# Four graph attention layers on one core: order and shape of the first loads and of the zero rows

## The chip, the core and the metric

The kernel runs on one core of one Trainium2 chip. The core has a matrix engine (TensorE, PE in the profile, with its weight loads as PEld), a vector engine (VectorE, DVE), an activation engine (ScalarE, ACT), GpSimd (POOL) and a queue engine that mostly issues transfers (SyncE, SP). ACT and POOL issue transfers too. Transfers of all three run on the core's 16 DMA engines. The metric is the device time of one execution in microseconds (us), the median of several runs; lower is better.

## The reference, cut to what matters

There are 4096 nodes with 256 features and one adjacency matrix for all four layers. Each layer normalises the nodes, applies ReLU, projects them, and replaces each node by a softmax-weighted sum over its neighbours, which is added to the node. Layer 0 has biases, layer 1 an ELU, layer 2 four heads, layer 3 a positive and a negative attention.

```python
h = jnp.maximum(_layernorm(x, axis=-1), 0.0)
x = x + _L0_gnn_ref(h, adj, L0_gnn_W, ...)   # layer 0; layers 1, 2, 3 in the same form
# inside a layer
h = node_features @ W.T + b_W
e = (h @ a1)[:, None] + (h @ a2)[None, :] + b_a[0]
e = jnp.where(e > 0, e, 0.2 * e)
attention = jax.nn.softmax(jnp.where(adjacency_matrix > 0, e, NEG_INF), axis=1)
h_prime = attention @ h
```

`adj` is int32, 4096 x 4096 (64 MB), and most of it is zero: the edge probability falls with the node's number, so that later nodes have few neighbours.

## The kernel before, in words

**Two paths.** `list_layers` (L468) does the work. A flag at its end says whether the lists that it built were long enough; if not, `dense_layers` would run. With these inputs the flag is zero, and only `list_layers` counts.

**Layer 0 is dense.** The targets are cut into NIB = 8 blocks of 512, the sources into NT = 32 tiles of 128. `block(ib)` (L1185) makes one `Unit` per block, with 32 steps, one for each source tile `jt`. Four source tiles are a chunk (CH = 4). At a chunk's first step `get` (L1189) issues the loads of the *next* chunk's adjacency (`load`, L1170: two transfers `s_raw` of 512 KB in the order of the SP queue, four buffers), turns this chunk's integers into bytes on DVE (L1201, `s_m`, or `mpre` for chunk 0), and, after chunk 0, writes them to DRAM as `mask_t` (L1203). Each step then needs the node tile's projected row `g[:, jt, :]`, so it forces the node work forward until `L0.ready[jt]` holds.

**A step's pipeline.** `run` (L1111) walks the plan with LEAD = (0, 2, 3, 6): a step is fetched at position p, weighed on DVE three positions later (L952, `s_p` = max of the two branches times the mask), and multiplied on PE six positions later (L988, `s_acc`). After each step it lets the queue `posts` move on by two parts and `lists_q` by one or two.

**Node work.** `node_rows` (L647) treats two tiles: statistics on DVE (L657, L658), 1/sqrt on ACT (L661, L662) and DVE (L673 to L675), the centred and clipped rows `s_z` (L666), the addition of the layer's bias to `x` on POOL (L670), two transposes per tile on PE (L680), and `project` (L693), which multiplies by the layer's weights `L.w` on PE (L702, `s_pj`) and scales the result on ACT (L713 to L737). It is a generator; a `yield` hands control back, and a number after it asks for that delay in the planner's own clock. `target_rows` (L873) makes `s_grow` for a block out of the scores of its four tiles.

**Weights.** `weights(l, pool, prep)` (L521) issues a layer's loads on the ACT queue (`s_w` L566, `s_wt` L574, `s_av` L576), and then at once the small products `s_wa` on PE (L580) and their copies into `L.w` on DVE (L592); for layer 0 also the bias row (L596 to L616). The tile `s_wt` has one buffer, so layer 1's waits for layer 0's to be used.

**The start of phase 0** (L1127 to L1230) is the part that the change touches. In order: all eight loads of `x` (512 KB each, 1 KB a row) on the ACT queue, with layer 0's weights after the first of them; layer 1's weights with their products; the constants of the list builder on POOL; then the zero rows. The zero rows are one extra row, number HALF = 2048, in each of the eight `mask_t` and in the three `table`s of layers 1 to 3, which the lists' empty places point at. They are written from POOL with 128 partitions of 4 bytes for each `mask_t` (L1145), and with 43 or 44 partitions of 24 or 48 bytes for each `table` (L1150). After that the first adjacency chunk is loaded, all 16 pairs of node tiles are put into `posts`, and `run` begins.

**After phase 0** the lists of neighbours are built between the blocks (`list_sources`, L773, with gathers of mask columns on POOL), and layers 1 to 3 take the first 512 targets densely and the others by their lists (L1243 on). These parts are not touched, save that `weights` has another signature.

The program's order gives the priority, and the compiler may put a ready instruction of an engine ahead of one that waits. Once placed, the instructions of one engine, and the transfers issued from one queue, start in their order.

Of the kernel before, what the change touches and what calls it, by code (L numbers as in the profile page):

```python
# [17 lines left out]
P = 128  # L18
# [449 lines left out]
def list_layers(ctx: ExitStack, tc: tile.TileContext, a: dict, out: bass.AP, flag):  # L468
# [49 lines left out]

    layers = {}

    def weights(l, pool, prep):  # L521

        L = layers[l] = Layer()
        L.l = l
        L.H, L.part = LH[l], PART[l]

        ncols = D + 3 * L.H + (D if l == 3 else 0)
        L.w = pool.tile([P, 2, ncols], F32, name=f"s_w{l}", tag=f"s_w{l}")
        L.s = small.tile([P, NT, L.H], F32, name=f"s_s{l}", tag=f"s_s{l % 2}", bufs=1)
        L.ready = [False] * NT  # L530
        L.bias = None
        L.table = table[l]
        q = nc.scalar
        if l == 2:
            for h in range(HEADS):
                q.dma_start(
                    L.w[:, :, h * DH : (h + 1) * DH],
                    a["L2_gnn_W"][h].rearrange("(c p) o -> p c o", p=P),
                )
            wt = prep.tile([DH, HEADS, D], F32, name="s_wt2", tag="wt")  # L540
            q.dma_start(wt, a["L2_WT"].rearrange("h o i -> o h i"))
            av = prep.tile([DH, HEADS, 2], F32, name="s_av2", tag="av")
            q.dma_start(av, a["L2_av"])
            ps = ps_mm.tile([P, 2, 2 * HEADS], F32, name="s_wa2", tag="mm")
            for c in range(2):
                for h in range(HEADS):
                    nc.tensor.matmul(
                        ps[:, c, 2 * h : 2 * h + 2],
                        lhsT=wt[:, h, c * P : (c + 1) * P],
                        rhs=av[:, h, :],  # L550
                        start=True,
                        stop=True,
                    )
            nc.vector.tensor_copy(L.w[:, :, D : D + HEADS], ps[:, :, 0 : 2 * HEADS : 2])
            nc.vector.tensor_copy(L.w[:, :, D + HEADS : D + 3 * HEADS : 2], ps[:, :, 1 : 2 * HEADS : 2])
            nc.vector.tensor_scalar(
                L.w[:, :, D + HEADS + 1 : D + 3 * HEADS : 2],
                ps[:, :, 1 : 2 * HEADS : 2],
                SLOPE - 1.0,
                None,  # L560
                op0=ALU.mult,
            )
            return L
        src, srcT = (("L0_WT", "L0_gnn_W"), ("L1_gnn_W", "L1_WT"), None, ("L3_gnn_W", "L3_WT"))[l]
        if l < 3:
            q.dma_start(L.w[:, :, 0:D], a[src].rearrange("(c p) o -> p c o", p=P))  # L566
        else:
            for k in range(2):
                q.dma_start(
                    L.w[:, :, k * (D + 6) : k * (D + 6) + D],  # L570
                    a["L3_gnn_wtrans"][k * D : (k + 1) * D, :].rearrange("(c p) o -> p c o", p=P),
                )
        wt = prep.tile([P, 2, D], F32, name=f"s_wt{l}", tag="wt")
        q.dma_start(wt, a[srcT].rearrange("(c p) i -> p c i", p=P))  # L574
        av = prep.tile([P, 2, 2], F32, name=f"s_av{l}", tag="av")
        q.dma_start(av, a[f"L{l}_av"])  # L576
        ps = ps_mm.tile([P, 2, 2], F32, name=f"s_wa{l}", tag="mm")
        for c in range(2):
            for k in range(2):
                nc.tensor.matmul(  # L580
                    ps[:, c, :],
                    lhsT=wt[:, k, c * P : (c + 1) * P],
                    rhs=av[:, k, :],
                    start=(k == 0),
                    stop=(k == 1),
                )
        for h in range(L.H):

            sign = (1.0, -1.0)[h]
            t = D + L.H + 2 * h  # L590
            for col, k, by in ((D + h, 0, sign), (t, 1, sign), (t + 1, 1, sign * (SLOPE - 1.0))):
                nc.vector.tensor_scalar(  # L592
                    L.w[:, :, col : col + 1], ps[:, :, k : k + 1], by, None, op0=ALU.mult
                )
        if l == 0:
            L.bias = prep.tile([1, D + 2], F32, name="s_bias0", tag="s_bias")  # L596
            q.dma_start(L.bias[:, 0:D], a["L0_bW_row"])
            ba = prep.tile([1, 1], F32, name="s_ba0", tag="ba")
            q.dma_start(ba, a["L0_ba"])
            bc = prep.tile([P, 2], F32, name="s_bc0", tag="bc")  # L600
            q.dma_start(bc, a["L0_bW_col"])
            pb = ps_mm.tile([1, 2], F32, name="s_pb0", tag="mm")
            for k in range(2):
                nc.tensor.matmul(
                    pb, lhsT=bc[:, k : k + 1], rhs=av[:, k, :], start=(k == 0), stop=(k == 1)
                )
            nc.vector.tensor_add(L.bias[:, D : D + 1], pb[:, 0:1], ba)
            nc.vector.tensor_copy(L.bias[:, D + 1 : D + 2], pb[:, 1:2])

            pb = ps_mm.tile([P, D + 2], F32, name="s_pbb", tag="mm")  # L610
            nc.tensor.matmul(pb, lhsT=ones[0:1, :], rhs=L.bias, start=True, stop=True)
            L.bias = const.tile([P, D + 3], F32, name="s_bias_all")
            nc.scalar.copy(L.bias[:, 0 : D + 2], pb)
# [3 lines left out]
        return L  # L617

# [28 lines left out]
    def node_rows(L, T0):  # L647
# [1 line left out]

        u = f"{L.l}_{T0}"  # L650
        tiles = (T0, T0 + 1)
        while any(stored[T] < L.l - 1 for T in tiles):
            yield
        mv = small.tile([P, 2, 2], F32, name=f"s_mv_{u}", tag="mv")
        for k, T in enumerate(tiles):
# [471 lines left out]
    with ExitStack() as phase:  # L1127
# [2 lines left out]
        stage = phase.enter_context(tc.tile_pool(name="s_stage", bufs=4))  # L1130
        mpool = phase.enter_context(tc.tile_pool(name="s_mask", bufs=5))
        gpool = phase.enter_context(tc.tile_pool(name="s_g0", bufs=1))
        for b in range(NIB):
            nc.scalar.dma_start(
                x[:, b * IT : (b + 1) * IT, :],
                a["x"][b * IB : (b + 1) * IB, :].rearrange("(c p) d -> p c d", p=P),
            )
            if b == 0:
                L0 = weights(0, prep, prep)
        L1 = weights(1, const, prep)  # L1140
        consts = list_constants(lists_p)
        zero_m = const.tile([P, 4], U8, name="zero_m")
        nc.gpsimd.memset(zero_m, 0.0)
        for b in range(NIB):
            nc.gpsimd.dma_start(mask_t[b][HALF : HALF + 1, :].rearrange("o (p k) -> (o p) k", k=4), zero_m)  # L1145
        zero = const.tile([P, 12], F32, name="zero")
        nc.gpsimd.memset(zero, 0.0)
        for l in (1, 2, 3):
            k = 12 if l == 3 else 6
            nc.gpsimd.dma_start(  # L1150
                table[l][HALF : HALF + 1, :].rearrange("o (p k) -> (o p) k", k=k), zero[0 : GW[l] // k, 0:k]
            )
        g0 = gpool.tile([P, NT, GW[0]], F32, name="g0")
# [10 lines left out]
        L1.pre = keep.tile([P, DP, GW[1]], F32, name="pre1")  # L1164
        L1.rows = rows_of(L1)
        half = CH // 2

        loaded = {}
# [1 line left out]
        def load(n):  # L1170

            ib, c = divmod(n, NCH)
            loaded[n] = []
            for h in range(2):
                raw = stage.tile([P, half, IB], I32, name=f"s_raw_{ib}_{c}_{h}", tag="raw")
                r0 = (c * CH + h * half) * P
                nc.sync.dma_start(
                    raw,
                    a["adjT"][r0 : r0 + half * P, ib * IB : (ib + 1) * IB].rearrange(
                        "(c p) i -> p c i", p=P  # L1180
                    ),
                )
                loaded[n].append(raw)

        def block(ib):  # L1185
            masks = {}
            seen = lists_p.tile([P, JT, IT], F32, name=f"seen_{ib}", tag="seen", bufs=2)

            def get(jt):  # L1189
                if jt % CH == 0:  # L1190
                    c = jt // CH
                    n = ib * NCH + c
                    if n + 1 < NIB * NCH:
                        load(n + 1)
                    m = (
                        mpre[:, :, ib * IB : (ib + 1) * IB]
                        if c == 0
# [21 lines left out]
                u.on_end = lambda: push(lists_q, list_sources(ib, seen, lists_p, consts))  # L1219
            return u  # L1220

        load(0)
        for T in range(0, NT, 2):
            push(posts, node_rows(L0, T))
        run([s for ib in range(NIB) for s in block(ib).plan()])
        push(lists_q, find_flag())
        while lists_q:
# [6 lines left out]
    gat = ctx.enter_context(tc.tile_pool(name="s_gather", bufs=9))  # L1234
    stream = ctx.enter_context(tc.tile_pool(name="s_stream", bufs=3))
    for l in (2, 3):
        L = weights(l, late, prep)
        L.pre = late.tile([P, DP, GW[l]], F32, name=f"pre{l}")
        L.rows = rows_of(L)
    for l in (1, 2, 3):  # L1240
        layers[l].big = late
    plan = []
# [147 lines left out]
```

## Time and profile before

| | |
|---|---|
| time | 1915.78 us (median of 3; 1912.8 to 1916.86) |
| span of the profiled execution | 1907.4 us |
| PE busy | 1753.6 us, 92% |
| PEld busy | 1481.6 us, 78% |
| DVE busy | 1361.7 us, 71% |
| POOL busy | 984.0 us, 52% |
| ACT busy | 606.4 us, 32% |
| moved by DMA | 253.30 MB, mean 133 GB/s |

The busy shares are means over the whole span. The profile also cuts the span into 40 equal slices (47.7 us each) and gives each engine's busy share in tenths, follows the chain of work that ended last, lists each line's instructions with what they waited for, and gives the bytes that the DMA engines moved in any stretch. A PE record's length includes its overlap with its neighbours, so a stretch's PE time is best read from how many matmuls start in it.

### The profile page before, as it was taken

How to read it: one execution, taken by the hardware profiler on the slowest of the kernel's cores; microseconds unless marked ns; L12 is line 12 of the kernel's file. 1: busy time of each engine (PE TensorE's matmuls, PEld its weight loads, DVE VectorE, ACT ScalarE, POOL GpSimd, SP SyncE). 2: the span in 40 equal slices, each digit the busy share in tenths (PEclk: the TensorE clock that was granted, in tenths of full speed). 3: DMA queues.
4: the chain of work that ended last, by engine and by line, in shares of the span. 5: the costliest groups of instructions: out<-in, count | busy, mean ns of one | idle time of the engine just before them, and what ended most of it. 6: DMA issues, size and time to landing. Idle time of an engine off the chain costs nothing.

```text
span 1907.4 us, 29989 instructions
## 1 busy us (share of the span) xinstructions
PE 1753.6 (92%) x9818; PEld 1481.6 (78%) x9818; DVE 1361.7 (71%) x3899; ACT 606.4 (32%) x1793; POOL 984.0 (52%) x962
## 2 busy tenths in 40 slices
PE   0299999999999888888889999999999999999997
PEld 0188888888888776667665778788999888888886
DVE  2286687787788434567668989989888466777775
ACT  0264111011011001123234776768999101111111
POOL 3120047754563376777764645444555177655542
PEclk9999999999999979999899999999999999999999
DMA  9832634753662233455432333333333366666653
GB/s 179 135 128 93 227 119 129 232 151 124 202 196 66 61 86 109 133 152 137 123 109 68 104 89 90 90 99 84 105 95 86 122 204 197 194 182 175 190 155 93
DMA packets 128760, 253.30 MB, mean 133 GB/s; under 512 B 22195, under 2 KB 51284, under 8 KB 128596
## 3 DMA queue, kind: packets, MB, share of 16 engines
q0 software_dynamic: 45696, 119.49, 23.6%
q1 hardware_dynamic: 74752, 125.23, 20.6%
q10 hardware_dynamic: 8148, 6.57, 2.3%
q8 instruction: 81, 1.33, 0.3%
q14 instruction: 83, 0.68, 0.1%
HBM read 215.32 MB, written 35.89 MB: 132 GB/s over the span
## 4 chain that ended last, share of the span: by engine, by line
PE 81%; DMA 8%; DVE 7%; issue 2%; ACT 1%; another core or an unknown queue 1%; POOL 1%; ACTq 0%; DVEq 0%; POOLq 0%
PE s_acc L988 50%; PE s_accm L1013 18%; PE s_pj L702 7%; DMA s_gg<-table,idx 4%; DVE s_p L952 3%; PE idx_ps L834 3%; DMA mask_t<-s_m 2%; PE s_sT L886 1%; PE s_tp L680 1%; DMA s_av<-in_L_av 1%; POOL s_gg L1289 1%; DVE first L828 1%; DVE s_st L657 0%; DVE s_p L961 0%
## 5 line engine op out<-in xcount | busy, mean ns | idle before, releaser
L1289 POOL DMA_INDIRECT s_gg<-table,idx x654 | 679.6, 1039 | 499.8 <-PE s_acc L988 191.5
L952 DVE SCALAR_TENSOR_TENSOR s_p<-s_grow,s_gg,mlist 128x128 f32<-128x128 f32 x1090 | 345.2, 346 | 187.1 <-DMA s_gg<-table,idx 128.2
L988 PE MATMUL s_acc<-g,s_p 128*128 128x257 f32 x2048 | 463.4, 382 | 0.0
L988 PEld LDWEIGHTS s_acc<-g,s_p 128*128 128x128 f32 x2048 | 384.9, 191 | 50.6
L847 POOL DMA_INDIRECT mlist<-mask_t,idx x218 | 265.5, 1218 | 277.5 <-DVE idx L844 214.4
L988 PE MATMUL s_acc<-s_gg,s_p 128*128 128x257 f32 x1308 | 310.0, 386 | 14.6 <-DVE s_p L952 14.2
L988 PEld LDWEIGHTS s_acc<-s_gg,s_p 128*128 128x128 f32 x1308 | 245.6, 192 | 60.3 <-DVE s_p L952 26.8
L952 DVE SCALAR_TENSOR_TENSOR s_p<-s_grow,g,s_m 128x512 f32<-128x512 f32 x224 | 166.4, 748 | 83.5 <-PE s_acc L988 64.1
L952 DVE SCALAR_TENSOR_TENSOR s_p<-s_grow,pre,mpre 128x128 f32<-128x128 f32 (+1 forms) x588 | 190.8, 364 | 43.0 <-PE s_acc L988 28.6
L1013 PE MATMUL s_accm<-s_p,s_gg 128*65 128x128 f32 x1744 | 202.5, 273 | 0.0
L938 ACT ACTIVATE s_p<-s_grow,s_minus,s_gg 128x128 f32<-128x128 f32 x436 | 187.1, 486 | 22.3 <-PE s_accm L1013 11.6
L1013 PEld LDWEIGHTS s_accm<-s_p,s_gg 128*65 128x65 f32 x1744 | 192.6, 138 | 1.9
L988 PE MATMUL s_acc<-pre,s_p 128*128 128x257 f32 x768 | 186.3, 387 | 0.6 <-DVE s_p L952 0.4
L892 ACT ACTIVATE s_grow<-s_sT 128x256 f32<-128x256 f32 (+2 forms) x127 | 45.1, 381 | 411.2 <-PE s_sT L886 361.6
L702 PE MATMUL s_pj<-s_w,s_hT 128*128 128x259 f32 (+3 forms) x640 | 168.8, 407 | 3.1 <-ACT s_g L737 2.6
L952 DVE SCALAR_TENSOR_TENSOR s_p<-s_grow,s_gs,s_ms 128x512 f32<-128x512 f32 x196 | 142.5, 747 | 38.5 <-PE s_accm L1013 18.0
L988 PEld LDWEIGHTS s_acc<-pre,s_p 128*128 128x128 f32 x768 | 145.3, 194 | 22.6 <-DVE s_p L952 0.9
L988 PE MATMUL s_acc<-s_gs,s_p 128*128 128x257 f32 x672 | 155.8, 385 | 0.2 <-DVE s_p L952 0.2
L702 PEld LDWEIGHTS s_pj<-s_w,s_hT 128*128 128x128 f32 x640 | 124.5, 202 | 27.3 <-ACT s_g L737 3.7
L988 PEld LDWEIGHTS s_acc<-s_gs,s_p 128*128 128x128 f32 x672 | 128.0, 192 | 21.4 <-DVE s_p L952 3.7
L1013 PE MATMUL s_accm<-s_p,pre 128*65 128x128 f32 (+1 forms) x928 | 120.6, 284 | 0.0
L1201 DVE TENSOR_SCALAR s_m<-s_raw 128x1024 uint8<-128x1024 int32 x112 | 78.0, 712 | 58.1 <-DMA s_raw<-in_adjT 57.4
(125 smaller groups left out, 1648.1 us busy)
## 6 DMA issues: line engine op xcount, KB each, us to landing
s_raw<-in_adjT SPq DMA_DIRECT2D x128, 512.0 KB, 5.6
mask_t<-s_m SPq DMA_DIRECT2D x56, 256.0 KB, 4.1
s_gs<-table SPq DMA_DIRECT2D x21, 516.0 KB, 5.7
s_gg<-table,idx POOLq DMA_INDIRECT x654, 3.4
table<-s_g SPq DMA_DIRECT2D x28, 258.0 KB, 2.3
s_ms<-mask_t SPq DMA_DIRECT2D x28, 256.0 KB, 3.6
x<-in_x ACTq DMA_DIRECT2D x8, 512.0 KB, 4.1
out<-s_out SPq DMA_DIRECT2D x32, 128.0 KB, 3.4
```

The lines of the kernel that those rows point to most:

```text
L680: nc.tensor.transpose(tp[:, c, :], zs[k][:, c * P : (c + 1) * P], ident)
L702: nc.tensor.matmul(ps, lhsT=hT[:, c, :], rhs=L.w[:, c, k * (D + 6) : k * (D + 6) + cols], start=(c == 0), stop=(c == 1),)
L828: nc.vector.tensor_tensor(first, place, lof[:, t, :].unsqueeze(1).to_broadcast([P, P, JT]), op=ALU.is_equal)
L834: nc.tensor.matmul(ps[:, 0:cap], lhsT=first[:, :, j], rhs=val[:, 0:cap, j * IT + t], start=(j == 0), stop=(j == JT - 1),)
L847: nc.gpsimd.indirect_dma_start(out=mlist[:, OFFS[T] + k, :], out_offset=None, in_=mask_t[ib], in_offset=bass.IndirectOffsetOnAxis(ap=idx[: ...
L892: nc.scalar.activation(grow[:, h1:h2, :], ps[:, h1 - h0 : h2 - h0].rearrange("p h a b -> p h (a b)"), AF.Exp, scale=scale,)
L938: nc.scalar.activation(w[:, h, :], u.grow[:, h, :], AF.Relu, scale=g[h][:, n - 1 : n], bias=minus)
L952: nc.vector.scalar_tensor_tensor(p[:, k, :], u.grow[:, h, :], g[k][:, n - 1 : n], m, op0=ALU.min if L.l == 3 and h == 1 else ALU.max, op1= ...
L988: nc.tensor.matmul(u.accs[it][h], lhsT=p[:, k, it * P : (it + 1) * P], rhs=g[k][:, 0:n], start=first, stop=last,)
L1013: nc.tensor.matmul(u.regions[h], lhsT=g[k][:, 0 : DH + 1], rhs=p[:, k, :],  start=first and (u.nt > 1 or h == 0), stop=last, skip_group_ch ...
L1201: nc.vector.tensor_scalar(m[:, h * half : (h + 1) * half, :], raw, 0.0, None, op0=ALU.is_gt)
L1289: nc.gpsimd.indirect_dma_start(out=g, out_offset=None, in_=L.table, in_offset=bass.IndirectOffsetOnAxis(ap=index[T][:, k : k + 1], axis=0),)
```

## The change

The change reorders and reshapes the start of phase 0.

- `weights` is split: it makes the tiles, and a generator `make_weights` first issues the loads on a queue `q` that the caller names, and after a `yield` does the products. A flag `L.made` says that the products are issued; `node_rows` of a layer waits for it.
- `x` is loaded block by block on the SP queue (`load_x`), and each block's two pairs of node tiles are put into `posts` with it. The order on SP is: x block 0, adjacency chunk 0, x blocks 1 to 3; x blocks 4 to 7 follow behind chunks 0 to 3 of the first block of targets.
- The zero rows are written at chunk 4 (`zero_rows`), on SP, from one partition: 512 bytes in one piece for each `mask_t`, and pieces of at most 258 floats (1032 bytes) for the tables: one, two (the second 24 bytes) and two.
- Layer 1's weights are loaded at chunk 5 on SP, and their products come into `posts` behind the node pairs.
- Layers 2 and 3 run their generators to the end where they did before.

It is meant to let the first matmuls start when their own inputs have come, without the transfers that are needed later.

```diff
-    def weights(l, pool, prep):
+    def weights(l, pool, prep, q):
...
-        q = nc.scalar
+        L.made = False
+        L.making = make_weights(L, pool, prep, q)
+        next(L.making)
+        return L
+
+    def make_weights(L, pool, prep, q):
+        l = L.l
...
         av = prep.tile([P, 2, 2], F32, name=f"s_av{l}", tag="av")
         q.dma_start(av, a[f"L{l}_av"])
+        if l == 0:
+            L.bias = prep.tile([1, D + 2], F32, name="s_bias0", tag="s_bias")
+            q.dma_start(L.bias[:, 0:D], a["L0_bW_row"])
...
+        yield 15.0
         ps = ps_mm.tile([P, 2, 2], F32, name=f"s_wa{l}", tag="mm")
...
-        return L
+        L.made = True
...
-        while any(stored[T] < L.l - 1 for T in tiles):
+        while any(stored[T] < L.l - 1 for T in tiles) or not L.made:
             yield
...
-        for b in range(NIB):
-            nc.scalar.dma_start(
+
+        def load_x(b):
+
+            nc.sync.dma_start(
                 x[:, b * IT : (b + 1) * IT, :],
                 a["x"][b * IB : (b + 1) * IB, :].rearrange("(c p) d -> p c d", p=P),
             )
-            if b == 0:
-                L0 = weights(0, prep, prep)
-        L1 = weights(1, const, prep)
-        consts = list_constants(lists_p)
-        zero_m = const.tile([P, 4], U8, name="zero_m")
-        nc.gpsimd.memset(zero_m, 0.0)
-        for b in range(NIB):
-            nc.gpsimd.dma_start(mask_t[b][HALF : HALF + 1, :].rearrange("o (p k) -> (o p) k", k=4), zero_m)
-        zero = const.tile([P, 12], F32, name="zero")
-        nc.gpsimd.memset(zero, 0.0)
-        for l in (1, 2, 3):
-            k = 12 if l == 3 else 6
-            nc.gpsimd.dma_start(
-                table[l][HALF : HALF + 1, :].rearrange("o (p k) -> (o p) k", k=k), zero[0 : GW[l] // k, 0:k]
-            )
+            for T in (b * IT, b * IT + 2):
+                push(posts, node_rows(L0, T))
+
+        def zero_rows():
+
+            zero = prep.tile([1, 2 * D], F32, name="zero", tag="wt")
+            nc.gpsimd.memset(zero, 0.0)
+            for b in range(NIB):
+                nc.sync.dma_start(mask_t[b][HALF : HALF + 1, :], zero[:, 0 : IB // 4].bitcast(U8))
+            for l in (1, 2, 3):
+                for k in range(0, GW[l], D + 2):
+                    n = min(D + 2, GW[l] - k)
+                    nc.sync.dma_start(table[l][HALF : HALF + 1, k : k + n], zero[:, 0:n])
+
+        L0 = weights(0, prep, prep, nc.scalar)
...
+        def behind(c):
+
+            if c + 4 < NIB:
+                load_x(c + 4)
+            if c == 4:
+                zero_rows()
+            if c == 5:
+                L1 = weights(1, const, prep, nc.sync)
+                L1.pre = keep.tile([P, DP, GW[1]], F32, name="pre1")
+                L1.rows = rows_of(L1)
+                push(posts, L1.making)
...
                     if n + 1 < NIB * NCH:
                         load(n + 1)
+                    if ib == 0:
+                        behind(c)
...
+        load_x(0)
         load(0)
-        for T in range(0, NT, 2):
-            push(posts, node_rows(L0, T))
+        for b in range(1, 4):
+            load_x(b)
+        consts = list_constants(lists_p)
+        for _ in L0.making:
+            pass
         run([s for ib in range(NIB) for s in block(ib).plan()])
```

More of the change, by code (lines that the diff above doesn't have):

```diff
@@ L562, in weights @@
             )
-            return L
+            L.made = True
+            return
         src, srcT = (("L0_WT", "L0_gnn_W"), ("L1_gnn_W", "L1_WT"), None, ("L3_gnn_W", "L3_WT"))[l]
@@ L576, in weights @@
         q.dma_start(av, a[f"L{l}_av"])
+        if l == 0:
+            L.bias = prep.tile([1, D + 2], F32, name="s_bias0", tag="s_bias")
+            q.dma_start(L.bias[:, 0:D], a["L0_bW_row"])
+            ba = prep.tile([1, 1], F32, name="s_ba0", tag="ba")
+            q.dma_start(ba, a["L0_ba"])
+            bc = prep.tile([P, 2], F32, name="s_bc0", tag="bc")
+            q.dma_start(bc, a["L0_bW_col"])
+        yield 15.0
         ps = ps_mm.tile([P, 2, 2], F32, name=f"s_wa{l}", tag="mm")
@@ L595, in weights @@
         if l == 0:
[L596 to L601, printed above, removed]
             pb = ps_mm.tile([1, 2], F32, name="s_pb0", tag="mm")
@@ L616, in weights @@
             )
-        return L
+        L.made = True
     posts, lists_q = [], []
@@ L1162, in rows_of @@
             return f
-        L1.pre = keep.tile([P, DP, GW[1]], F32, name="pre1")
-        L1.rows = rows_of(L1)
         half = CH // 2
@@ L1236, in list_layers @@
     for l in (2, 3):
-        L = weights(l, late, prep)
+        L = weights(l, late, prep, nc.scalar)
         L.pre = late.tile([P, DP, GW[l]], F32, name=f"pre{l}")
         L.rows = rows_of(L)
+        for _ in L.making:
+            pass
     for l in (1, 2, 3):
```

## The prediction

> **What bounds the kernel now.** I read the page's 40 slices first, because a change at the start must show there or nowhere. Each digit is a busy share in tenths of a 47.7 us slice.
>
> ```profile
> PE   0299999999999888888889999999999999999997
> ...
> DMA  9832634753662233455432333333333366666653
> GB/s 179 135 128 93 227 119 129 232 151 124 202 196 66 61 86 109 133 152 137 123 109 68 104 89 90 90 99 84 105 95 86 122 204 197 194 182 175 190 155 93
> ```
>
> PE is empty in slice 1 and nearly empty in slice 2, then full in nearly all. PE is the bound, but it starts late. DMA is 9 tenths busy in slice 1, yet moves a mean of 179 GB/s. Stretches of 4 and 8 us show why (columns: stretch, length, busy time and instructions of PE, PEld, DVE, ACT and POOL, clock, DMA share, GB/s):
>
> ```profile
> 4.00:8.00 4.00, 0.00 (x0) 0.00 (x0) 2.93 (x7) 0.00 (x0) 4.00 (x3) 1.00 1.06 375
> 8.00:12.00 4.00, 0.23 (x2) 0.26 (x2) 1.33 (x5) 0.00 (x0) 0.99 (x7) 1.00 1.08 372
> 20.00:24.00 4.00, 0.00 (x0) 0.00 (x0) 1.06 (x3) 0.00 (x0) 3.08 (x6) 1.00 1.00 305
> 28.00:36.00 8.00, 0.00 (x0) 0.00 (x0) 0.00 (x0) 0.00 (x0) 0.56 (x1) 1.00 1.00 18
> 52.00:60.00 8.00, 0.00 (x0) 0.00 (x0) 0.00 (x0) 0.00 (x0) 0.00 (x0) 1.00 1.10 26
> 72.00:76.00 4.00, 0.00 (x0) 0.00 (x0) 2.22 (x14) 1.28 (x8) 0.00 (x0) 1.00 0.93 313
> ```
>
> The engines move 372 GB/s, fall to 18 to 26 while still counted as fully busy, and recover only at 72 us. The fall follows the zero rows: POOL issues eight from 18.21 to 23.1 us and three more up to 46.83. This is how long they take (the transfers' table of the first 90 us: KB each, median us to landing):
>
> ```profile
> mask_t<-zero_m POOLq DMA_DIRECT2D x8, 0.5 KB, 22.5
> table<-zero POOLq DMA_DIRECT2D x1, 1.0 KB, 41.4
> ```
>
> Half a kilobyte takes 22.5 us, one kilobyte 41.4. They are 8 x 128 pieces of 4 bytes and 43 + 44 + 43 of 24 or 48 bytes, 1154 in all. From 18.2 to 72.2 us that is 54 us, 47 ns a piece. Last, the chain of waits in order of time (start us, us, what):
>
> ```profile
> 19.72 39.97 DMA mask_t<-s_m
> ...
> 60.08 12.23 another core or an unknown queue
> ...
> 72.33 7.63 DMA s_av<-in_L_av
> ...
> 80.10 1.84 PE s_wa L580 x8
> 81.94 1.14 PE s_tp L680 x4
> 83.08 3.68 PE s_pj L702 x8
> ...
> 98.61 0.87 PE s_acc L988 x4
> ...
> 111.29 1.82 PE s_pj L702 x8
> 113.12 3.04 PE s_acc L988 x14
> 116.15 0.44 PE s_tp L680 x4
> ```
>
> PE stands at layer 1's `s_wa` (80.10), which nobody needs before layer 0's first block ends. It waits there 63.0 us for `s_av`, which sits behind layer 1's other weights, these behind `x` on the ACT queue, and all behind the zero rows. The first node tiles (81.94) stand behind it in PE's order. ACT is caught as well: its first `s_r` (L661) comes at 72.8, after 55.3 us idle, behind those transfers. The first `s_acc` is at 98.6. From there to 200 us PE is busy 101.34 of 101.40 us: what the first `s_acc` gains, the end gains.
>
> **The Trainium skill.** "DMA: Bandwidth & Descriptors", Specifications, asks at least 512 B a transfer for line rate and says that smaller ones are read, modified and written. The 47 ns a piece and the 18 GB/s agree with a heavy price; no run yet separates the zero rows from their neighbours. The same page, "Issuing engines are not separate DMA queues", says that transfers of all queues share the 16 engines; so moving `x` from ACT to SP buys no bandwidth, only another order. The trace agrees: POOL's few bytes slow SP and ACT. "TensorE: Matmul & The Clock Gate", Part 1, says that PE runs at half clock after idling. The trace agrees in effect: eight `s_pj` take 3.68 us at 83 us and 1.82 at 111. The new start pays this once, as the old one did.
>
> **Part by part.**
>
> *Layer 0's weights without `x` ahead.* Before, `s_av` was issued at 2.42 and landed at 11.64, with x block 0 (0.52 MB), `s_w` and `s_wt` (0.52 MB) ahead on ACT's queue and SP's adjacency beside them. Now x block 0 goes to SP. If the queues share evenly, `s_av` waits for 0.52 MB and as much of SP's: 1.05 MB at 372 GB/s is 2.8 us. The flow builds up over the first 4 us (147 GB/s on average), so `s_av` should land at about 7. Bounds: 5.5 (nothing in the way) and 11.6 (as before).
>
> *The products and the bias row.* From the first `s_wa` at 11.77 to the end of the bias product `s_pbb` at 17.06 were 5.3 us, cold then as it will be. That puts the end at 12.3. x block 0 is first on SP and lands at 5 to 6, so statistics and `s_z` of the first pair (3 to 4 us of DVE: two at 0.4, 0.1 and 0.35 each) are ready in time.
>
> *First node tiles to first `s_acc`.* Before, 81.94 to 98.61 = 16.7 us. I take the same: 12.3 + 16.7 = 29.0. Bounds: 24 (`s_av` at 5.5 and some transposes ahead of the bias row, about 3 us) and 34 (`s_av` as before: 17.1 + 16.7). Gain at the first `s_acc`: 98.6 - 29 = 69.6 us.
>
> *Will PE stay fed?* A pair of node tiles costs PE 5.73 us in steady state (transposes at 110.42 and again at 116.15), a chunk twice that, 11.5 us. A chunk must move 1.05 MB of adjacency, 0.26 of mask and now 0.52 of `x`: 1.83 MB, or 4.9 us at 372 GB/s. By 29 us some 9 MB could have moved; chunks 0 and 1 and x blocks 0 to 4 with the weights are 5.2. DVE did 26.5 us of work before 100 us (15.2 to 80, 11.3 to 100) and 47.5 from 98.6 to 165, about 74 for the first block, against 16 x 5.73 = 92 of PE. ACT is at 7.6 of 11.5 in a chunk. None bounds.
>
> *Zero rows at chunk 4, on SP.* 13 issues. An SP or POOL issue takes 0.34 to 0.54 us in the trace: 4.4 to 7.0 us of SP. The adjacency of the next chunk is issued ahead of them, in the same step, and that after it a chunk (11.5 us) later; a load lands in 4.2 to 5.6 us, so SP may be held some 6 us beyond its own work without PE noticing. The pieces themselves: no row of before shows a write of one long piece. Low bound: 13 pieces at 47 ns, under 1 us of the engines; high bound: each cut into sixteen, 208 pieces, 9.8 us. I take the low one, hidden either way by one chunk of prefetch or nearly.
>
> *Layer 1's weights at chunk 5.* Three issues on SP (0.37 each in the trace). `s_wt` shares its buffer with `zero`, so SP waits there until the zero writes have read it; behind it on SP stand `s_av` and chunk 5's mask write, which nobody awaits soon, then the adjacency of chunk 7. The page's fit of 2.0 us fixed per small transfer is my estimate for the wait; hidden. The products (1.84 us cold, less when warm) are moved, not removed. The wait on `L.made` holds nothing: layer 1's node rows come after the first block, some 30 us later.
>
> *The rest* (L2 and L3 weights, lists) is shifted whole. Cost 0, with 3 us for reordering.
>
> Sum: 1915.8 - 69.6 = **1846.2**, the forecast.
>
> **Rivals.**
>
> 1. *The new start isn't primed.* Before, DVE used the stall to do 26.5 us of work ahead; now that lies beside the first chunks. For it: DVE is at 11.14 of 11.5 us in the stretch from 103 to 114.5. Against it: that stretch is catching up, and the next ones show 8.73, 7.76, 7.34. If half falls on the path: 1846 + 13 = 1859.
> 2. *The small pieces aren't the cause, or the collapse comes back at chunk 4.* For it: the trace shows only that they coincide. Against it: bandwidth was 372 to 378 GB/s with `x`, weights and adjacency together before the first of them. A stall of 54 us less 6 hidden: 1846 + 48 = 1894.
> 3. *The whole stall moves (slower).* It recurs, layer 1's loads queue behind it on SP as they did on ACT (60.08 to 79.96, 20 us), the compiler puts `s_wa` early in PE's order, and PE must fill its pipeline again (16.7): 1846 + 54 + 20 + 17 = 1937. For it: the same PE order was chosen before. Against it: the products now come into `posts` behind all node pairs.
>
> **How the numbers follow.** Main case 0.74 (1838 to 1854, by the bounds 24 and 34 and the 3 us); rival 1 0.15; rival 2 0.08; rival 3 0.03. The range takes in the main case and rival 1, below with PE noise and above with half-hidden zero rows and the 9.8 us bound: 1834 to 1872. Slower is rival 3, no change the gap between rivals 2 and 3, 0.01; faster is the rest, 0.96.
>
> **What would show it.** First `s_acc` near 29 us instead of 98.6; GB/s above 300 through the first 20 us and no stretch under 50 with DMA full; `s_wa` waiting under 10 us in its first use and not at all in its second; PE busy from 30 us on, with transposes 5.73 us apart; the zero rows landing in a few us. A gap on PE near 75 to 100 us, with DVE waiting for `s_raw`, would mean rival 2; DVE as releaser of the first `s_acc` groups, rival 1. It would be wrong if `x` blocks 1 to 3 delay adjacency chunk 1 beyond 35 us, or if PE's order still holds layer 1's products near the front.

## The result, and the profile after

| | before | after |
|---|---|---|
| time, median | 1916.3 us (1912.8 to 1917.3) | 1842.1 us (1839.7 to 1842.7) |
| ratio | | 0.961, 95% interval 0.960 to 0.963 |
| span of the profiled execution | 1907.4 us | 1840.9 us |
| first `s_acc` on PE | 98.6 us | 29.9 us |
| end of the first block of targets (first copy `den<-s_acc`) | 183.2 us | 115.4 us |

The change makes the kernel 3.9% faster, by 74.3 us; 1846.2 was forecast. The profile after is read in the order in which before was read. First the page's 40 slices, now of 46.0 us:

```profile
PE   6999999999998888988899999999999999999997
...
DMA  7644646635622334454423233333332567656652
GB/s 257 235 154 143 196 121 182 208 108 176 214 58 63 79 108 134 133 152 123 117 66 104 75 93 106 82 91 103 104 94 76 158 204 210 194 171 184 185 153 88
```

PE is six tenths busy in slice 1, where it was empty, and full or nearly so from slice 2 on. The DMA engines are *less* busy in slice 1 than before (7 against 9) and move more (257 GB/s against 179). From slice 12 on the row of GB/s (58 63 79 108 134) repeats that of before from slice 13 on (66 61 86 109 133), some 66 us earlier. The stretches of the start (columns as before: stretch, length, busy time and instructions of PE, PEld, DVE, ACT and POOL, clock, DMA share, GB/s; a packet's whole time and bytes are counted in the stretch in which it starts, so a share can exceed 1):

```profile
4.00:8.00 4.00, 0.00 (x0) 0.00 (x0) 1.89 (x7) 0.30 (x1) 4.00 (x4) 1.00 1.08 385
8.00:12.00 4.00, 2.01 (x12) 1.92 (x12) 1.49 (x9) 0.04 (x1) 0.49 (x4) 1.00 1.11 343
...
28.00:36.00 8.00, 7.99 (x38) 6.41 (x38) 8.00 (x15) 6.74 (x27) 4.38 (x4) 1.00 0.80 263
52.00:60.00 8.00, 8.00 (x42) 6.71 (x41) 7.34 (x23) 4.94 (x19) 2.19 (x4) 1.00 0.78 267
...
28.00:200.00 172.00, 171.89 (x867) 148.24 (x868) 131.68 (x306) 63.96 (x234) 27.62 (x28) 1.00 0.53 174
```

Where before moved 18 and 26 GB/s with its DMA engines counted as full, after moves 263 and 267 with them at 0.80 and 0.78. PE is busy for 171.89 of the 172 us from 28 to 200. Before was as full once it had begun:

```profile
98.60:200.00 101.40, 101.34 (x495) 86.75 (x494) 71.69 (x185) 54.45 (x199) 17.31 (x23) 1.00 0.39 123
```

The chain of waits in order of time (start us, us, what):

```profile
1.90 7.63 DMA s_av<-in_L_av
9.67 1.85 PE s_wa L597 x8
...
14.60 1.15 PE s_tp L691 x4
15.75 3.76 PE s_pj L713 x8
...
29.87 0.87 PE s_acc L999 x4
...
41.71 0.44 PE s_tp L691 x4
...
47.45 0.44 PE s_tp L691 x4
...
103.42 0.79 PE s_wa L597 x8
```

PE waits once for the first `s_av`, and never for layer 1's: its `s_wa` comes at 103.42, near the end of the first block, and takes 0.79 us where the first takes 1.85. The zero rows are the second and third line of SP's timeline (start us, us, engine, line, what):

```profile
39.36 1.65 SPq L1188 DMA_DIRECT2D s_raw<-in_adjT  x2
41.11 4.34 SPq L1159 DMA_DIRECT2D mask_t<-zero  x8
45.49 1.43 SPq L1163 DMA_DIRECT2D table<-zero  x5
...
47.41 0.97 SPq L1188 DMA_DIRECT2D s_raw<-in_adjT  x2
```

They hold SP for 5.8 us, ahead of them the next chunk's adjacency is out already, and PE doesn't notice. From the first `s_acc` to the end are 1811.0 us (1840.9 less 29.9), and were 1808.8 (1907.4 less 98.6): everything gained was gained ahead of the first `s_acc`. The 2.2 us that the part behind it is longer come from one profile each, and what makes them isn't shown.

### The profile page after: what moved, and what is told of

It is laid out like the page before. It is cut to its first block, busy times and chain, and to the rows that moved or that the text cites. A ratio compares the mean times of both kernels' runs of the same rounds, so it can differ in the third digit from the quotient of the medians.

```text
span 1840.9 us, 29987 instructions
## 1 busy us (share of the span) xinstructions
PE 1751.7 (95%) x9818; PEld 1479.2 (80%) x9818; DVE 1362.7 (74%) x3899; ACT 607.2 (33%) x1793; POOL 990.1 (54%) x950
## 3 DMA queue, kind: packets, MB, share of 16 engines
q10 hardware_dynamic: 3236, 1.84, 0.4%
## 4 chain that ended last, share of the span: by engine, by line
PE 86%; DVE 5%; DMA 4%; issue 2%; ACT 1%; POOL 1%; ACTq 0%; DVEq 0%; POOLq 0%
PE s_acc L999 51%; PE s_accm L1024 21%; PE s_pj L713 7%; DMA s_gg<-table,idx 4%; PE idx_ps L845 3%; DVE s_p L963 2%; PE s_tp L691 1%; PE s_sT L897 1%; POOL s_gg L1320 1%; DMA s_av<-in_L_av 1%; DVE first L839 1%; PE s_oT L1086 0%; DVE s_z L677 0%; DVE s_st L668 0%; DVE x L1053 0%
## 5 line engine op out<-in xcount | busy, mean ns | idle before, releaser
L1320 POOL DMA_INDIRECT s_gg<-table,idx x654 | 689.4, 1054 | 491.3 <-PE s_acc L999 187.7
L963 DVE SCALAR_TENSOR_TENSOR s_p<-s_grow,s_gg,mlist 128x128 f32<-128x128 f32 x1090 | 344.7, 345 | 187.3 <-DMA s_gg<-table,idx 115.4
L999 PE MATMUL s_acc<-s_gg,s_p 128*128 128x257 f32 x1308 | 308.2, 384 | 16.7 <-DVE s_p L963 16.5
L999 PE MATMUL s_acc<-s_gs,s_p 128*128 128x257 f32 x672 | 157.3, 387 | 0.2 <-DVE s_p L963 0.2
L1024 PEld LDWEIGHTS s_accm<-s_p,pre 128*65 128x65 f32 x928 | 104.1, 138 | 17.8 <-issue 14.0
```

The lines of the kernel that those rows point to most:

```text
L963: nc.vector.scalar_tensor_tensor(p[:, k, :], u.grow[:, h, :], g[k][:, n - 1 : n], m, op0=ALU.min if L.l == 3 and h == 1 else ALU.max, op1= ...
L999: nc.tensor.matmul(u.accs[it][h], lhsT=p[:, k, it * P : (it + 1) * P], rhs=g[k][:, 0:n], start=first, stop=last,)
L1024: nc.tensor.matmul(u.regions[h], lhsT=g[k][:, 0 : DH + 1], rhs=p[:, k, :],  start=first and (u.nt > 1 or h == 0), stop=last, skip_group_ch ...
L1320: nc.gpsimd.indirect_dma_start(out=g, out_offset=None, in_=L.table, in_offset=bass.IndirectOffsetOnAxis(ap=index[T][:, k : k + 1], axis=0),)
```

## The experiments

The change does four things at once: it loads in another order, moves the zero rows later and to SP, writes them in large pieces, and moves layer 1's products in PE's order. The theory on which the forecast stood: the tiny pieces make the DMA collapse, and PE's order only decides who is hit. The first rival: the crowd of early loads makes it, and the order of need cures it. The second: PE's order is the loss, whatever the transfers do.

Eight of the twelve runs below (all but the one with only the mask rows tiny, the fourth layout, and the last two) were on chips where the kernel before takes some 2100 us, with a granted clock of 0.94 to 0.95 (0.98 in the result above). Both kernels are slower there behind the start: from 200 to 400 us, PE is busy 178.8 us in before, where it is 199.8 in the profile of before above. The starts agree, though: the first block of before ends at 186.0 us there and at 183.2 here, that of after at 114.7 and 115.4. So effects on the start are compared by the end of the first block in us, times only as a ratio to before on the same chip. (The times in the recorded expectations are for the first chip; divided by 1916 they are ratios.) Each end of a block is read from one profile. The end of the first block is the first of the two times in the group of copies out of `s_acc`, for before and after on the slower chips:

```profile
L1039 DVE COPY den<-s_acc x12: 138/140/152, 186.0 to 347.2; 128x1 f32<-128x1 f32 x12
```

```profile
L1050 DVE COPY den<-s_acc x16: 138/140/152, 114.7 to 359.3; 128x1 f32<-128x1 f32 x16
```

**Both kernels again**, unchanged, as the measure for the others.

> The kernel before, unchanged, for a second profile: its profiled execution took 1909.2 us where the timed ones took a median of 1916. If the stall at the start varies, the first s_acc is not at 98.6 us but some us later (about 106), and the rest from there to the end is the same 1809 us within 2. If the stall is fixed, the difference lies after it.

> The changed kernel itself once more, as the base for the three scratch kernels of this call on the same chip: first s_acc at 29.9 us, bandwidth above 340 GB/s up to 20 us, and 66 to 76 us below the kernel before.

Measured: before 2104.3 us in one execution, with its first `s_acc` at 101.31, where about 106 was expected of a longer stall; the 1809 us expected behind it can't be tested on this slower chip, where 2001 follow. After: 2027.3 us, ratio 0.969 (0.958 to 0.980), first `s_acc` at 29.19, as expected. The stall of before isn't of one length: the mask write in its chain lands after 45.02 us, where it took 39.97 in the first profile, on the other chip.

```profile
20.30 45.02 DMA mask_t<-s_m
...
86.20 1.84 PE s_wa L580 x8
101.31 0.87 PE s_acc L988 x4
```

**The old order with few pieces.** Before, with only the shape of the zero rows changed; they stay on POOL, where they were.

```diff
-            nc.gpsimd.dma_start(mask_t[b][HALF : HALF + 1, :].rearrange("o (p k) -> (o p) k", k=4), zero_m)
+            nc.gpsimd.dma_start(mask_t[b][HALF : HALF + 1, :], zero[:, 0 : IB // 4].bitcast(U8))
...
+            n = GW[l] // (4 if l == 3 else 2)
+            for k in range(0, GW[l], n):
+                nc.gpsimd.dma_start(table[l][HALF : HALF + 1, k : k + n], zero[:, 0:n])
```

> The kernel before with one edit: the zero rows go out in few pieces, still from GpSimd and still at the start (512 bytes a mask row; table rows in pieces of 516 or 528 bytes; as compiled 16 runs of 32 bytes a mask row and 3 to 12 runs a table piece, some 170 runs instead of 1154). Theory A, the many tiny pieces choke the DMA engines: bandwidth stays above 300 GB/s until x, layer 1's weights and the first adjacency chunks are in (about 11 MB at 372 GB/s, some 30 us), the second product s_wa starts at about 32 us, the first s_acc at about 49, and the time is about 1866 us (1855 to 1880). Theory B, the order of the loads does it and the zero rows are only coincident: about 1916 us, with the stall unchanged.

Measured: 2043.9 us, ratio 0.966 (0.958 to 0.973; expected 0.968 to 0.981). The first block ends at 137.9, 48.1 us earlier than in before on this kind of chip, and the span of the profiled execution is 49.5 shorter (2053.1 against 2102.6). Stretches, then the chain:

```profile
24.00:28.00 4.00, 0.00 (x0) 0.00 (x0) 0.69 (x1) 0.00 (x0) 3.60 (x8) 1.00 1.08 386
28.00:36.00 8.00, 0.00 (x0) 0.00 (x0) 3.90 (x18) 1.27 (x8) 2.53 (x4) 1.00 1.07 372
```

```profile
29.37 6.91 DMA s_av<-in_L_av
36.41 1.84 PE s_wa L580 x8
...
53.24 1.08 PE s_acc L988 x4
```

The collapse is gone with all early loads in place: the crowd alone doesn't make it. What remains is the order: PE still stands at layer 1's `s_wa`, until 36.41, since the whole of `x` is ahead of it on the ACT queue at full rate. I expected 32 and 49 for the two marks; full rate moves what is queued some 4 us later than I had counted. From the trace's packets, POOL's write of a 512-byte row from one partition went out as 16 runs of 32 bytes, so "few pieces" were 128 here for the masks, not 8; that didn't matter.

**The new order with tiny pieces, late and early.** The first writes the old shapes at chunk 4 on SP, the second the old shapes at the old place on POOL, ahead of the first step.

```diff
         def zero_rows():
-                nc.sync.dma_start(mask_t[b][HALF : HALF + 1, :], zero[:, 0 : IB // 4].bitcast(U8))
+                nc.sync.dma_start(mask_t[b][HALF : HALF + 1, :].rearrange("o (p k) -> (o p) k", k=4), zero_m)
```

> The changed kernel with the zero rows in the old shape (128 pieces of 4 bytes a mask row, 43 or 44 of 24 or 48 bytes a table row) at chunk 4 on the SP queue. Theory A: the bandwidth falls under 50 GB/s from about 41 us for some 50 us; PE runs on what it has (chunks 4 and 5, two times 11.5 us) and then stands for about 30 us: about 1873 us (1855 to 1895). Theory B, only the place at the start mattered: 1842 us, within 5.

> The changed kernel with the zero rows in the old shape and at the old place (from GpSimd, behind the list constants, at about 15 us), all the rest of the new order kept. Theory A: the collapse comes back at about 16 us with only the first transfers in; PE gets through one to two chunks and stands until about 70 us: about 1890 us (1870 to 1905), so that the new order alone is worth 10 to 45 us. Theory B, PE's order and the loads' order did it: 1842 us, within 5.

Measured late: 2049.4 us, ratio 0.972 (0.967 to 0.978; expected 0.968 to 0.989), the first block ends at 139.2, 24.5 us later than after. Early: 2072.6 us, 0.982 (0.977 to 0.987; expected 0.976 to 0.994), 157.3, 42.6 us later; the profile is of its fastest execution, 2050.5 us. Two stretches of the late kernel, which issues its mask rows from 41.28 us on:

```profile
52.00:60.00 8.00, 2.09 (x10) 1.49 (x8) 0.90 (x2) 0.00 (x0) 0.35 (x1) 0.88 0.00 0
60.00:68.00 8.00, 2.24 (x6) 1.11 (x6) 1.45 (x5) 2.45 (x9) 0.00 (x0) 0.50 0.01 0
```

and two of the early one, which issues them from 14.87:

```profile
20.00:24.00 4.00, 2.85 (x13) 1.94 (x13) 3.89 (x21) 3.84 (x17) 0.00 (x0) 1.00 0.77 24
36.00:44.00 8.00, 0.00 (x0) 0.00 (x0) 0.00 (x0) 0.00 (x0) 0.00 (x0) 0.50 0.37 2
```

The loss follows the pieces to either place, in the late kernel after 40 us of smooth work. The picture is not the same, though. In the early kernel the few packets that start from 36 to 44 us (six in the trace) take some 8 us each, where packets took a mean of 0.06 us from 16 to 20 us. In the late one hardly a packet starts from 46 to 72 us: the DMA share is 0.00 there, not full. In that time SP's queue sends nothing more. Its timeline:

```profile
41.28 7.46 SPq L1159 DMA_DIRECT2D mask_t<-zero_m  x8
67.36 6.58 SPq L1164 DMA_DIRECT2D table<-zero  x3
```

SP stands 18.6 us at the tables' rows, until a mask row has landed, and the next adjacency stands behind them. So in the late kernel the tiny rows land late and SP's order adds to it; the runs don't part the two. ACT, too, stands from 51.72 for 11.2 us at an instruction with an unknown releaser.

With the kernels above this makes a table of two by two (end of the first block, us):

| | tiny pieces | few pieces |
|---|---|---|
| old order | 186.0 | 137.9 |
| new order (tiny: early) | 157.3 | 114.7 |

The shape alone brings 48.1, the order alone 28.7, together 71.3. That the two sum to more (76.8) isn't enough to say that they overlap: there is one profile for each cell, and the stall's length varies (183.2 and 186.0 for two profiles of before). And the new order with few pieces is after itself, with the zero rows late and on SP; early on POOL, few pieces weren't tried in the new order.

**Which of the tiny pieces?** As the early kernel, but with only the eight mask rows tiny and early; the tables are written large and late, as in after.

> e3_small_early with only the masks' zero rows in tiny pieces at the start; the tables' rows go in large pieces at chunk 4 as in the changed kernel. If the masks' 1024 pieces make the stall: block end at 145 to 157 us (157.3 in e3_small_early). If the tables' 130 pieces do: at 115 to 117 us.

Measured: 1885.1 us against 1912.6 of before on this chip, ratio 0.985 (0.978 to 0.992); the first block ends at 159.6 (145 to 157 was expected if the masks make the stall, 115 to 117 if the tables do). The tables' 130 pieces aren't needed: the 1024 of 4 bytes are enough for all of it.

**What about these pieces?** After, with eight extra writes of 128 pieces ahead of the first step, issued on POOL into scratch memory that nothing reads. Four layouts:

```diff
+        # 1: adjacent rows of 512 bytes, 128 pieces of 4 bytes in each
+            nc.gpsimd.dma_start(scr[b : b + 1, :].rearrange("o (p k) -> (o p) k", k=4), z_s)
+        # 2: each piece of 4 bytes in a row of its own
+            nc.gpsimd.dma_start(scr[b * P : (b + 1) * P, 0:4], z_s)
+        # 3: pieces of 32 bytes, 16 in a row
+            nc.gpsimd.dma_start(scr[b * 8 : (b + 1) * 8, :].rearrange("r (p k) -> (r p) k", k=32), z_s)
+        # 4: as 1, but row HALF of eight tensors of 4097 x 512 bytes (the shape of mask_t)
+            nc.gpsimd.dma_start(scr[b][HALF : HALF + 1, :].rearrange("o (p k) -> (o p) k", k=4), z_s)
```

> The changed kernel with eight extra transfers from GpSimd at about 15 us into a scratch tensor that nothing reads: each 128 pieces of 4 bytes that fill one row of 512 bytes, as the old zero rows did for the masks. If the tiny pieces are the cause: the collapse is back (under 50 GB/s for 40 to 50 us), +30 to +55 us over the changed kernel. If only the tables' rows, or writes into the masks' own tensors, made it: no change.

> As m1_same_row, but each piece of 4 bytes goes to the head of a row of its own, 512 bytes apart. Theory S, pieces queue because they share one row's memory words: no collapse, within 6 us of the changed kernel. Theory N, the number of writes under some size counts wherever they go: as m1_same_row.

> As m1_same_row with the same 1024 pieces, but of 32 bytes each, sixteen to a row of 512 bytes. Theory S with a small word (32 bytes or less): no collapse, within 6 us. Theory S with a word of 512 bytes: sixteen pieces queue instead of 128, a collapse of an eighth, some 6 us, hidden. Theory N: as m1_same_row.

> m1_same_row with its eight rows not next to each other but each in a scratch tensor of the masks' own shape (4097 x 512 bytes), at the row that the masks' zero row has, so some 2 MB apart. Nothing else is written to or read from them. If the distance of the rows is what turns a slowdown of 10 us into a stall: the stall comes back, the block end at 135 to 160 us. If not (the tables' pieces, or the masks' own traffic, are needed): at 115 to 117 as in m1_same_row.

| layout | end of the first block | time | ratio |
|---|---|---|---|
| after | 114.7 | 2027.3 | 0.969 (0.958 to 0.980) |
| 1: adjacent rows | 115.5 | 2025.3 | 0.966 (0.952 to 0.980) |
| 2: own rows | 115.4 | 2020.0 | 0.963 (0.947 to 0.980) |
| 3: 32 bytes | 116.7 | 2037.2 | 0.972 (0.958 to 0.985) |
| 4: rows of eight tensors | 167.6 | 1890.0 (other chip) | 0.988 (0.979 to 0.996) |

(After ends its first block at 115.4 on a chip of the fourth's kind.) The first three cost the block 0.7 to 2.0 us. Layout 1 was expected to bring the collapse back, at 30 to 55 us, if tiny pieces as such were the cause: a miss. With no collapse there, the theories that layouts 2 and 3 were to part, S and N, have nothing to explain. So neither the number of pieces nor their 4 bytes are a price by themselves. Layout 1, where the extra writes only lower the bandwidth for some 10 us:

```profile
20.00:24.00 4.00, 2.67 (x13) 1.83 (x13) 3.88 (x6) 3.84 (x18) 4.00 (x7) 1.00 0.99 80
24.00:28.00 4.00, 3.58 (x14) 2.35 (x13) 4.00 (x20) 2.69 (x10) 1.58 (x2) 0.79 0.37 66
28.00:36.00 8.00, 7.91 (x36) 6.04 (x35) 8.00 (x15) 6.57 (x26) 3.46 (x3) 0.89 0.79 216
```

Layout 4, with the same pieces from the same engine at the same time:

```profile
20.00:24.00 4.00, 2.67 (x13) 1.74 (x12) 3.79 (x6) 3.84 (x18) 4.00 (x7) 1.00 1.58 72
28.00:36.00 8.00, 3.34 (x16) 2.56 (x16) 7.68 (x14) 2.58 (x10) 3.34 (x3) 0.99 2.50 17
44.00:52.00 8.00, 0.00 (x0) 0.00 (x0) 0.00 (x0) 0.00 (x0) 0.00 (x0) 0.63 0.49 2
```

The stall is back; the block's end is even later than the 135 to 160 us that were expected. It needs the place of the eight rows, each in a tensor of 2.1 MB, and not only the shape of the writes. The other chip isn't the reason: the kernel with all tiny pieces early stalled on the first kind of chip, the one with the mask rows alone on this kind. Nor is it the tiny packets' own recorded time that fills the engines. The queues' table from 10 to 110 us, first of layout 1, then of 4 (packets, MB, share of the time of 16 engines; q1 holds SP's transfers, q0 POOL's):

```profile
q1 hardware_dynamic: 13380, 21.91, 70.2%
...
q0 software_dynamic: 256, 0.00, 0.3%
```

```profile
q1 hardware_dynamic: 8322, 12.24, 99.4%
q0 software_dynamic: 256, 0.00, 2.0%
q14 instruction: 3, 0.02, 1.4%
```

Of 16 engines over 100 us (1600 us), POOL's packets take 32 us in layout 4. SP's take 1590 us for 8322 packets, 191 ns each, where they took 84 ns in layout 1 (1123 us for 13380). A packet's time runs from its start to its end, waits included: the loss shows in everyone else's packets, those of the instructions too, but what an engine does meanwhile isn't recorded.

**Layer 1's weights early again.** After, with layer 1's weights loaded on ACT and their products made ahead of the node tiles, as before.

```diff
+        L1 = weights(1, const, prep, nc.scalar)
+        for _ in L1.making:
+            pass
...
-            if c == 5:
-                L1 = weights(1, const, prep, nc.sync)
```

> The changed kernel with layer 1's weights again at the start, on ACT behind layer 0's, and their products again ahead of the node tiles in PE's order; everything else of the change stays. Read by the end of the first block of targets (first copy of its denominators on DVE: 114.7 us in the changed kernel, 186.0 in the kernel before, on this kind of chip). If PE's order was only the place where PE stood, and the slow transfers what it stood for: s_wt may go once its buffer is free at 11.5 us, lands some 5 us later, node tiles start at 19 instead of 14.6: block end at 118 to 121. If the order itself was a large part of the loss: 130 or later.

Measured: 1845.7 us against 1912.6, ratio 0.964 (0.958 to 0.971). The first block ends at 118.4, 3.0 us later than after. The chain:

```profile
8.99 1.84 PE s_wa L597 x8
...
18.74 1.84 PE s_wa L597 x8
...
33.76 0.87 PE s_acc L999 x4
```

As expected. PE has the old order, second `s_wa` ahead of the first node tiles, and it costs 3 us, with healthy transfers and `x` on SP. So PE's order alone isn't the loss: it says *where* PE stood, the transfers *how long*. Together with the whole of `x` ahead on the ACT queue it is worth more: the old order with few pieces ends its first block 23.2 us later than after (137.9 against 114.7).

**All of `x` at the front.** After, with x blocks 4 to 7 ahead of chunk 1 instead of behind chunks 0 to 3.

> The changed kernel with all eight blocks of x in front of adjacency chunk 1 on SP instead of four in front and four between the chunks. 2.1 MB more ahead of chunk 1 at 372 GB/s are 5.6 us; chunk 1 was turned into bytes at 22.5 us after landing by 17, so it would come at about 22 to 23. If x between the chunks matters: block end 3 to 6 us later (118 to 121). If not: within 1.5 us of 114.7.

Measured: 1837.6 us against 1912.6, ratio 0.960 (0.954 to 0.967); first `s_acc` at 27.65, first block at 113.2, 2.2 us *earlier* than after. I expected 3 to 6 later: a miss. Loading `x` between the chunks brings nothing that can be measured here. Nor is this kernel shown to be faster than after: the ratios' intervals overlap, and the first `s_acc` varies among kernels with the same start anyway (29.87 in after, 29.19 when it ran again, 30.81 in the late kernel).

## Why the prediction was right, point by point

**The main step held: the gain is what the first `s_acc` gains.** 68.7 us in the profiles (98.6 less 29.9) where 69.6 was forecast, and PE is fed from there on, with transposes 5.7 us apart (41.71 to 47.45). Which of the change's four parts earns it, the forecast couldn't say; that is what the experiments added. Its own terms were off in both directions:

| term | forecast | measured | |
|---|---|---|---|
| layer 0's `s_av` lands | 7 | 9.5 (1.90 + 7.63) | too early by 2.5 |
| first `s_wa` to the bias row | 5.3 | 4.9 (9.67 to 14.60) | |
| first node tiles to first `s_acc` | 16.7 | 15.3 (14.60 to 29.87) | too long by 1.4 |
| first `s_acc` | 29.0 | 29.9 | |

**The mis-sized term is `s_av`.** The step was that `s_av` waits for 0.52 MB of its own queue and as much of SP's. What the queues had moved by 9.5 us (packets, MB, share of 16 engines; q1 is SP's, q10 ACT's):

```profile
q1 hardware_dynamic: 1424, 1.93, 61.5%
q10 hardware_dynamic: 739, 0.53, 17.5%
```

ACT's queue had moved the 0.53 MB that was counted, but SP's 1.93 MB: the queues didn't share evenly. The measured 9.5 lies within the bounds given (5.5 to 11.6). That the whole came out only 0.9 us late is partly luck: the shorter path behind `s_av` made up for more than half of it.

**Zero rows at chunk 4.** Forecast 4.4 to 7.0 us of SP, hidden; measured 5.8 us, PE not held. The low value for the pieces themselves (13 at 47 ns, 0.6 us) was the right choice: the trace has 13 packets, one of 512 bytes for each mask row, with 0.4 us in sum. The buffer that layer 1's `s_wt` shares with `zero` cost no wait to speak of: SP issued `s_wt` at 49.08, 0.18 us after the issue ahead of it. The 2.0 us that stood for this wait are stated in the Trainium skill, "DMA: Bandwidth & Descriptors", Anatomy of one DMA, for transfers issued from GpSimd, not from SP, and no run here shows them.

**Layer 1's products.** Forecast: moved, no wait. Right, at 0.79 us instead of 1.84.

**The step that was wrong: 47 ns a piece.** It divided 54 us by 1154 pieces, and took the quotient for a price. (Even the 54 us weren't all stall: the engines moved 305 GB/s up to 24 us, and a mean of 104 from 60 to 72.) Layout 1 has 1024 such pieces and loses under a microsecond of block time, layout 4 has the same and loses 52.2 (167.6 less 115.4). So there is no price of a piece; the cost of the same pieces went from nearly nothing to 52 us with the place of their rows. The forecast didn't suffer, because the change takes these writes away, and the quotient served only for the 13 late pieces, where it came to under 1 us. That was luck.

**What the size of the transfers doesn't explain.** The Trainium skill, "DMA: Bandwidth & Descriptors", Specifications, on the read and write back of transfers under 512 B, isn't enough to explain it: layouts 1 to 3 are all under 512 B and harmless. The same page's "Latency and other measured facts" says that copies of large tiles slow down where rows lie 2 MiB or more apart in HBM (207 GB/s at 512 KiB, 164 at 2 MiB), and calls a clash of memory channels an inference. Here a spacing by tensors of 2.1 MB made the difference too, but the loss is of another order (2 to 27 GB/s from 24 to 76 us in layout 4), for writes of 4 bytes, and no trace shows the addresses. That the rows of eight tensors meet in one place of the memory is therefore argued, not shown.

**The rivals.** Rival 1, a start that isn't primed: DVE is indeed busy for 8.00 of 8.00 us from 28 to 36, but PE for 7.99; it brought no loss. Rival 2's second half was what the late tiny pieces tried: 24.5 us at the block's end, not the 48 that I gave it: the bandwidth was near zero for 26 us there (46 to 72), not 54, and PE worked on until 54. The sign given for it (DVE waiting for `s_raw`) wasn't what stopped PE first: PE waited 9.6 us for ACT, and ACT for an unknown releaser. Rival 3 needed the same, and the large pieces took it away.

**The medians gained more than the profiles.** Taking the profiled executions by their times, 1909.2 and 1842.6, the gain is 66.6 (68.7 less the 2.2 behind the first `s_acc`, rounded); the medians say 74.3. The difference is on the side of before: its profiled execution was 7.1 us quicker than its median. The stall's length varies (in the second profile of before, the mask write in the chain took 5.0 us longer and the first `s_acc` came 2.7 us later); but that profile is of another chip, and there is none of a 1916 us execution, so this is argued. The forecast took a gain read from one execution and subtracted it from the median of several: against the medians it was 4.7 us too cautious, against the profiles 3.0 us too bold.

## What to carry to other kernels

When a stretch shows the bandwidth at a twentieth, with the DMA engines full (or, as in the late kernel, empty while a queue waits for small writes to land), ask which small writes went out just before, and where they land, before reordering the loads: changing only their shape gave 48 of the 71 us here. Don't price tiny pieces by dividing a stall by their number; put them alone into a healthy kernel, in the memory layout of the real one, and look at what *others'* packets take. And products that wait for late transfers do not belong ahead of the first useful work in an engine's order: it cost 3 us when the transfers came soon, and PE stood there until 36.4 us when the whole of `x` was queued ahead of them.

## What the runs showed of the hardware that I had not expected

**The stall outlasts the writes.** In layout 4 the trace's packets of the extra writes run from 19.5 to 36.4 us, 128 packets of 32 bytes that hold eight pieces of 4 bytes each. In layout 1 the same packets are done by 26.9, in layout 2 by 21.7. But the stall of layout 4 goes on until 76 us, 40 us after the last of them is recorded as done. Whether the bytes had landed by then isn't in this trace; in the late kernel, SP was held until 67.36, 4.4 us after the last packet of the mask rows was recorded as done. The old order with few pieces also sent 128 packets of 32 bytes to the mask rows, each one run instead of eight pieces and read from one partition instead of 128, and kept 372 to 386 GB/s: 128 packets of 32 bytes to these rows are not enough for the stall. Pieces of 32 bytes in as large a number, spread over tensors like layout 4's, and other spacings were not tried.

**An engine waits with its inputs there.** ACT's timeline in layout 4, at a projection's scaling:

```profile
59.25 0.35 ACT L724 ACTIVATE g<-s_pj,s_bias_all,s_r 128x1 f32<-128x1 f32 x1 [20.21 <-remote]
```

ACT stood 20.21 us at it, and its input from PE had been there since about 40 us. The packets of the instruction queues were slow in the stall: 8 KB took 0.3 to 0.6 us in after, and 9.1, 10.0 and 3.2 us for the three in layout 4 that start at 26 to 29 us; from 10 to 110 us they take 1.4% of the engines' time instead of 0.2%. The slowest of them ends at 37.26, and an earlier wait of ACT, 5.69 us with the same unknown releaser, ends at 37.74. That fits a wait for instructions, but which engine's they were isn't recorded. For the wait of 20.21 us up to 59.25 the trace has no packet of these queues under way, so its cause stays open, as does that of the 12.23 us at 60.08 in the chain of before. The Trainium skill, "DMA: Bandwidth & Descriptors", Back-pressure in remote DMA, says that writes that are held up also hold up the engine's other queues. It says so of writes between cores; SP's 191 ns a packet in layout 4 look the same for writes to the core's own memory, but the mechanism isn't shown.
